# Another order of a layer's pieces, and another end of the recurrence, in a fused convolution-attention-recurrence kernel

## The chip, the cores and the metric

The kernel runs on one core of one Trainium2 chip. The metric is the device time of one execution in microseconds, as the median of several runs. The engines are TensorE (PE in the profile, its weight loads PEld), VectorE (DVE), ScalarE (ACT), GpSimd (POOL) and SyncE (SP, which here only issues transfers).

## The reference

The input x has 4 images of 128 channels and 64 x 64 pixels, all in float32. Two layers follow each other.

Layer 0 normalises over the channels, adds a 3 x 3 depthwise convolution with edge padding to the result, cuts each image into windows of 16 x 16, and lets each pixel of a window attend to its 5 x 5 neighbours, in two branches of four heads of 32 channels:

```
y = layernorm2d(x);  y = y + cpe(y)
q, k, v = per window and branch: Wq y, Wk y, Wv y
o = softmax over 25 neighbours (q . k_nb / sqrt(32)) . v_nb     # padding counts as zero logits
x = x + (Wo o of branch 0 + 0.5 * Wo o of branch 1) / sqrt(1.25)
```

Layer 1 takes the pixels as 4096 tokens of 128 features:

```
t = t + linear_attention(ln(t))      # elu + 1 features; cumulative sums over the tokens; num / den
t = t + ffn(ln(t)), where ffn is:
  Wx = x W^T, normalised per feature over all 4 * 4096 tokens, times gamma, plus beta
  y_t = sigmoid(Wx_t + V y_(t-1))    # a recurrence over the 4096 tokens of an image
```

The last normalisation needs the mean and the variance over all tokens of all images. So the recurrence can't begin until the last token's product is there.

## The kernel before

**Bands.** An image is worked in 4 bands of 16 rows (1024 tokens), 16 bands in all, and a band in 4 windows, 64 in all (`places`). The matmuls are float32, and each shows in the profile as two passes.

**Layer 0.** `norm_rows(n)` normalises a band's rows, turns them with TensorE and writes them into `ypad`. `convolve(n, half)` applies nine taps to two windows at a time, the first on ACT (L376), eight on DVE (L378), and copies the result to `y2w` on ACT (L414). Band 0 is different: `convolve_first` does windows 0 and 1 with taps on ACT and DVE, and `multiply_first` does windows 2 and 3 with matmuls against diagonal matrices (L396). A window then goes through `q`, `k`, `v` (L427, L440; `v` also sends two transfers, `v_sb`), `logits` (L467, L480, then four exponentials, L489), `sums` (L509, the softmax denominators; the copy `den`, L512, and the transfer `dc`), `values` (L524), `inverse` (DVE adds and inverts, L535 and L537, then the transfers `rd` and `rden` spread the result) and `scaled` (POOL, L552). `output0` (L578, L585) is the projection of half a band and needs all four windows of the band scaled.

**Layer 1.** Each band has two halves of 512 tokens. In the orders they are called `a` and `c`; the halves of the band before are `y` and `z` (in the last part `v` and `w` for the one before these). Per half the pieces are `output`, `measure`, `norm`, `turn`, `queries`, `keys`, `values`, `scores`, `turn_keys`, `accumulate` (the running state), `attend0`, `attend1`, `measure_last`, `send`, `spread`, `keep` and `product`. `send` and `spread` pass the second normalisation's factors through DRAM to all partitions. `keep` turns the result, copies it on ACT and stores it (L719). `product` multiplies by the recurrence's weights, and takes the statistics with DVE's `bn_stats` (L740) from `wx` in SBUF. The last half uses `norm_last` and `turn_last` in place of the factors (L616, L730).

**The order.** It is written out by hand. `START` writes out the order of pieces up to the fourth window. Then a loop goes through the windows with `SLOT`; numbers in it are gaps, and in the gaps of four windows the 24 entries of `LAYER1` are done one after the other, and steps of the next band's `front` (rows and taps) as `AHEAD` says. `TAIL` writes out what is left after the last window's logits. `warm.N` puts N matmuls on zeros ahead of the next piece that takes a PSUM bank. The order of the program is held on PE, DVE, ACT and POOL by `in_order()`; SP's queue isn't held by it. A piece that was done already is passed over:

```python
        if h is not None and name not in h.done:
            does[name](h)
            h.done.add(name)
```

**The recurrence.** Each image's 4096 tokens are cut into 128 segments of 32 steps, which run side by side as 512 columns; 11 steps ahead of the segment's own start, the first of them without a predecessor, make its first value. A step is three groups of columns: DVE seeds PSUM with the normalised product (L942), TensorE adds V y (L1004), ACT takes the sigmoid (L1009). The results of four steps make a block `ys`, from a ring of 3 buffers. For images 0 and 1 a block goes to the output by an accumulating transfer from POOL's queue (L1016), onto the residual that `keep` stored there. For images 2 and 3 the residual is loaded back (`res`, L913), added on POOL (L1022; the last step on DVE) and stored from SP's queue (L1028). At the end DVE compares segment ends with the warm-up's values (L1035), a flag is made from it (L1049), every engine loads it and branches (L1052, L1054) past a slower general version.

## Time and profile before

| | us |
|---|---|
| runs of the kernel before | 838.75, 839.15, 840.38; median 839.15 |
| the profiled execution's own time | 843.62 |
| its span | 841.80 |
| busy PE, DVE, ACT, POOL | 806.6, 693.2, 530.8, 254.2 |
| first layer 1 output (L578) | 72.0 |
| last window's logits done | 724.65 |
| first matmul of the recurrence (L1004) | 784.95 |
| last sigmoid begins | about 828.1 |

The profile is one execution; its times count from the span's start. A line such as L378 is a line of the kernel, and in a group `out<-in` names the tiles. What stands in square brackets after an instruction is the idle time of its engine before it and what ended it.

### The profile page before, as it was taken

The numbers are of one execution on the slowest core, as the hardware profiler recorded it, in microseconds if no ns is written. First come the engines' busy times: TensorE is split into PE (matmuls) and PEld (weight loads), VectorE is DVE, ScalarE is ACT, GpSimd is POOL, SyncE is SP. The second block draws the span as 40 slices with busy tenths as digits, with TensorE's granted clock in tenths as the row PEclk, the third lists the DMA queues.
The fourth block names the chain that finished last, engine by engine and source line by source line (L and its number), as shares of the span: only waits on it lengthen the run. The fifth ranks groups of instructions, "written<-read, shape, count | busy, mean of one in ns | idle before, by whom it ended". The sixth has DMA issues, their size and how long they took to land.

```text
span 841.8 us, 28915 instructions
## 1 busy us (share of the span) xinstructions
PE 806.6 (96%) x11803; PEld 642.3 (76%) x11805; DVE 693.2 (82%) x2127; ACT 530.8 (63%) x1026; POOL 254.2 (30%) x365
## 2 busy tenths in 40 slices
PE   6998999999999999999999999999999999988993
PEld 3766787878787878778787878787878878756792
DVE  6565989897989998998989898998999886466882
ACT  3675757676757576666767676757666665613782
POOL 2122232423233232413142323323332303121193
PEclk7999999999999999999999999999999999999997
DMA  4022141332323231414132232323141313121697
GB/s 140 18 64 70 42 113 42 79 79 66 91 68 97 57 103 36 109 42 119 40 86 75 62 87 67 96 65 98 39 108 39 92 41 95 44 56 38 209 224 174
DMA packets 81422, 68.81 MB, mean 82 GB/s; under 512 B 44800, under 2 KB 63872, under 8 KB 81280
## 3 DMA queue, kind: packets, MB, share of 16 engines
q1 hardware_dynamic: 53200, 43.47, 18.0%
q10 hardware_dynamic: 26928, 19.20, 9.2%
q0 software_dynamic: 1152, 4.19, 2.9%
q8 instruction: 95, 1.56, 0.8%
q14 instruction: 47, 0.39, 0.2%
HBM read 39.51 MB, written 17.89 MB: 68 GB/s over the span
## 4 chain that ended last, share of the span: by engine, by line
PE 86%; DVE 4%; DMA 4%; POOL 2%; ACT 1%; issue 1%; ACTq 0%; DVEq 0%; POOLq 0%; SPq 0%
PE bank L427 12%; PE bank L509 7%; PE bank L480 7%; PE bank L625 7%; PE bank L578 7%; PE bank L524 6%; PE bank L440 6%; PE bank L302 5%; PE bank L641 4%; PE z L1004 4%; PE bank L679 3%; PE bank L662 3%; PE bank L698 3%; PE bank L700 3%; PE bank L733 3%; PE bank L467 2%
## 5 line engine op out<-in xcount | busy, mean ns | idle before, releaser
L378 DVE SCALAR_TENSOR_TENSOR y<-ypad,cpe_w,y 128x512 f32<-128x512 f32 x240 | 191.7, 799 | 12.7 <-ACT y L376 7.7
L489 ACT ACTIVATE es<-bank 128x512 f32<-128x512 f32 x256 | 132.2, 604 | 32.1 <-PE bank L480 31.7
L285 POOL TENSOR_SCALAR rs<-mv 128x4 f32<-128x4 f32 (+2 forms) x100 | 25.3, 253 | 390.8 <-DVE mv L283 389.1
L552 POOL TENSOR_TENSOR oT<-o_sb,rden 128x512 f32<-128x512 f32 x64 | 83.0, 1297 | 119.1 <-DMA rden<-rd 104.2
L286 POOL TENSOR_TENSOR rs<-rs,mhalf 128x4 f32<-128x4 f32 (+2 forms) x100 | 106.0, 1060 | 8.3
L524 PEld LDWEIGHTS bank<-es,v_sb 128*32 128x32 f32 x3072 | 62.9, 110 | 39.2 <-issue 21.3
L480 PEld LDWEIGHTS bank<-q,k 32*64 32x64 f32 x4096 | 75.4, 130 | 2.7
L480 PE MATMUL bank<-q,k 32*64 32x96 f32 (+1 forms) x4096 | 77.5, 274 | 0.0
L512 ACT COPY den<-bank 128x512 f32<-128x512 f32 x64 | 37.4, 584 | 55.8 <-PE bank L509 55.3
L524 PE MATMUL bank<-es,v_sb 128*32 128x96 f32 (+1 forms) x3072 | 69.5, 237 | 1.6 <-DMA v_sb<-v_sb 1.6
L578 PEld LDWEIGHTS bank<-woT,oT 128*128 128x128 f32 x512 | 61.0, 196 | 13.2 <-POOL oT L552 9.6
L509 PE MATMUL bank<-es,ones 128*32 128x512 f32 x512 | 69.6, 605 | 0.6 <-ACT es L489 0.6
L427 PE MATMUL bank<-y2w,wqT 128*128 128x256 f32 x256 | 67.4, 386 | 2.4 <-DVE y2w L378 2.2
L625 PE MATMUL bank<-xl,awT 128*128 128x512 f32 x128 | 66.6, 607 | 0.0
L578 PE MATMUL bank<-woT,oT 128*128 128x128 f32 x512 | 62.3, 281 | 4.5 <-POOL oT L552 4.5
L427 PE MATMUL bank<-y2w,wkT 128*128 128x256 f32 x256 | 65.9, 380 | 0.0
L440 PE MATMUL bank<-wvT,y2w 128*128 128x256 f32 x256 | 65.9, 380 | 0.0
L535 DVE TENSOR_TENSOR dc<-dc,pad_c 128x32 f32<-128x32 f32 x64 | 25.5, 399 | 47.8 <-DMA dc<-den 47.7
L435 ACT COPY k<-bank 128x512 f32<-128x512 f32 x64 | 38.6, 603 | 41.2 <-PE bank L427 41.2
L627 ACT ACTIVATE low<-bank,minus 128x512 f32<-128x512 f32 x64 | 43.8, 685 | 24.5 <-PE bank L625 23.4
L427 PEld LDWEIGHTS bank<-y2w,wkT 128*128 128x128 f32 x256 | 47.3, 190 | 13.4 <-issue 7.5
L629 DVE SCALAR_TENSOR_TENSOR f<-low,bank 128x512 f32<-128x512 f32 x64 | 43.5, 680 | 16.6 <-ACT low L627 16.6
(131 smaller groups left out, 1687.9 us busy)
## 6 DMA issues: line engine op xcount, KB each, us to landing
rden<-rd SPq DMA_DIRECT2D x64, 256.0 KB
v_sb<-v_sb SPq DMA_DIRECT2D x128, 64.0 KB
factors<-factors ACTq DMA_DIRECT2D x31, 256.0 KB
xin<-in_xt SPq DMA_DIRECT2D x15, 512.0 KB
out<-rs_o ACTq DMA_DIRECT2D x16, 256.0 KB
resd<-rs_o ACTq DMA_DIRECT2D x16, 256.0 KB
out<-ot SPq DMA_DIRECT2D x32, 128.0 KB
out<-ys POOLq DMA_DIRECT2D x8, 512.0 KB, 7.4
```

What stands on the lines that cost most here:

```text
L286: nc.gpsimd.tensor_tensor(rs[:, :n], rs[:, :n], mhalf[:, :n], ALU.pow)
L378: nc.vector.scalar_tensor_tensor(y2, src, cpe_w[:, tap : tap + 1], y2, ALU.mult, ALU.add)
L427: nc.tensor.matmul(pps[:, br * WT : (br + 1) * WT], wT[:, br * P : (br + 1) * P], y2, start=True, stop=True,)
L440: nc.tensor.matmul(vps[:, e * 256 : (e + 1) * 256], y2[:, e * P : (e + 1) * P], wvT, start=True, stop=True,)
L480: nc.tensor.matmul(sps[h][half * KC : (half + 1) * KC, cols], w["k"][rows, k0 : k0 + KC], w["q"][rows, cols], start=False, stop=br == BR - ...
L489: nc.scalar.activation(es, sps[h], AF.Exp, scale=scale)
L509: nc.tensor.matmul(dps[rows], ones[:, :HD], w["es", h], start=True, stop=True)
L524: nc.tensor.matmul(ops[rows, cols], w["v"][:, n, c0 : c0 + HD], w["es", h][:, cols], start=(br, n) == pieces[0], stop=(br, n) == pieces[-1],)
L552: nc.gpsimd.tensor_tensor(oTs[n][:, :, :, wj * WS : (wj + 1) * WS], w["o"].rearrange("p (a r c) -> p a r c", a=BR, c=WS), w["rden"].rearra ...
L578: nc.tensor.matmul(yps[:, j * P : (j + 1) * P], oT[:, br, t], woT[:, br, :], start=br == 0, stop=br == BR - 1,)
L625: nc.tensor.matmul(zps, awT[:, m * P : (m + 1) * P], h.xl, start=True, stop=True)
L627: nc.scalar.activation(low, zps, AF.Exp, bias=minus)
```

## The change

Three things change. First, the order: `LAYER1`, one entry of `AHEAD`, `START` and `TAIL` are written anew, with the same pieces. In `LAYER1` values.a moves up beside queries.a, queries.c beside keys.c and attend1.a beside attend0.a, measure_last of the second half moves to the end of its own round, and keep.z stands ahead of norm.a. In `START`, `prepare` comes first, and the first parts of mul.2 and mul.3 stand ahead of q.0; there are 11 `warm` matmuls instead of 5. In `TAIL`, there are 14 instead of 13, scaled.63 and output.a come earlier, and product.z stands ahead of turn_last.c.

Second, the last statistics are taken from PSUM, ahead of the copy to `wx`, which DVE makes instead of ACT; the aggregate and the scale follow at once, and the shift takes one operation fewer.

Third, the last block of images 0 and 1 is not accumulated by the transfer. Its residual is loaded into `end_a`, DVE adds each of the last four steps to it, and ACT's queue stores it plainly. The ring of blocks has 4 buffers, and the last `ot` is added on POOL like the others.

```diff
@@ -41,55 +41,55 @@
 NA = B * NH // 2
 TOL = 5e-7
 LAYER1 = (
-    "measure_last.z",
+    "",
     "",
     "product.y send.z output.a",
     "measure.a spread.z output.c",
-    "norm.a",
-    "measure.c keep.z",
-    "",
-    "turn.a norm.c",
+    "keep.z norm.a",
+    "measure.c",
+    "turn.a",
+    "norm.c",
     "",
     "",
-    "keys.a product.z",
-    "turn.c queries.a",
-    "values.a",
-    "turn_keys.a scores.a keys.c",
-    "accumulate.a values.c",
-    "turn_keys.c attend0.a queries.c",
-    "attend1.a",
+    "queries.a values.a turn.c",
+    "product.z keys.a",
+    "turn_keys.a",
+    "scores.a keys.c queries.c accumulate.a",
+    "values.c",
+    "turn_keys.c attend0.a attend1.a",
+    "",
     "scores.c",
-    "measure_last.a",
-    "accumulate.c keep.a send.a",
+    "measure_last.a keep.a",
+    "accumulate.c send.a",
     "",
     "",
     "attend0.c spread.a attend1.c",
-    "",
+    "measure_last.c",
 )
 SLOT = ("sums", "values", "logits", 0, "scaled", "inverse", 1, "q", 2, 3, "k", "v", 4, 5)
-AHEAD = ("03", "01223345", "001245", "00234")
+AHEAD = ("03", "01223345", "001455", "00234")
 START = (
-    "warm.5 conv.0 prepare q.0 front conv.1 mul.2 mul.3",
-    "mul.2 k.0 front v.0 q.1 k.1 logits.0 front",
-    "q.2 front front front front mul.3 v.1 front",
-    "logits.1 sums.0 k.2 values.0 v.2 front front front",
-    "inverse.0 front front load.2 front logits.2 q.3 front",
-    "front sums.1 scaled.0 front values.1 inverse.1 q.4 k.4",
-    "sums.2 k.3 front front front v.3 scaled.1 logits.3",
-    "values.2 v.4 inverse.2 front front",
+    "prepare conv.0 front warm.3 mul.2 conv.1 mul.3 q.0",
+    "k.0 front front mul.2 v.0 q.1 k.1 front",
+    "logits.0 q.2 front front mul.3 front front v.1",
+    "sums.0 logits.1 front values.0 front front front k.2",
+    "inverse.0 scaled.0 v.2 front front load.2 front logits.2",
+    "front sums.1 front values.1 q.3 warm.6 sums.2 inverse.1",
+    "q.4 k.3 v.3 warm.2 front logits.3 scaled.1 front",
+    "values.2 inverse.2 front k.4 front v.4 front",
 )
 TAIL = (
-    "scaled.61 keep.w output.y send.w sums.63 spread.w output.z measure.z",
-    "measure.y inverse.62 norm.z values.63 product.w norm.y turn.y scaled.62",
-    "keys.y queries.y scores.y turn_keys.y inverse.63 turn.z values.z values.y",
-    "queries.z keys.z accumulate.y warm.1 attend0.y turn_keys.z product.v attend1.y",
-    "measure_last.y scores.z accumulate.z send.y spread.y attend0.z attend1.z keep.y",
-    "measure_last.z warm.2 send.z scaled.63 product.y warm.10 output.a measure.a",
-    "output.c measure.c norm.a spread.z keep.z turn.a norm.c turn.c",
-    "queries.a queries.c keys.a values.a keys.c turn_keys.a values.c scores.a",
-    "accumulate.a attend0.a attend1.a scores.c turn_keys.c measure_last.a accumulate.c keep.a",
-    "attend0.c send.a attend1.c measure_last.c spread.a keep.c norm_last.c product.a",
-    "turn_last.c product.z product.c",
+    "warm.2 warm.4 output.y keep.w send.w scaled.61 spread.w sums.63",
+    "measure.y output.z measure.z norm.z product.w norm.y warm.2 inverse.62",
+    "turn.z turn.y values.63 queries.y keys.y scores.y scaled.62 turn_keys.y",
+    "inverse.63 values.z values.y keys.z accumulate.y attend0.y queries.z turn_keys.z",
+    "attend1.y measure_last.y send.y product.v scaled.63 warm.3 spread.y accumulate.z",
+    "keep.y scores.z attend0.z attend1.z measure_last.z output.a send.z measure.a",
+    "product.y output.c measure.c norm.a turn.a keep.z norm.c values.a",
+    "keys.a turn.c warm.1 warm.1 spread.z queries.a warm.1 keys.c",
+    "turn_keys.a values.c scores.a accumulate.a attend0.a turn_keys.c queries.c attend1.a",
+    "measure_last.a scores.c accumulate.c keep.a attend0.c attend1.c send.a measure_last.c",
+    "spread.a keep.c norm_last.c product.a product.z turn_last.c product.c",
 )
 DGROUP = 4
 TINY, HUGE = 1e-30, 1e30
@@ -232,6 +232,9 @@
     stats = const.tile([P, B * T // 512, 6], F32, name="stats")
 
     wx = const.tile([P, B, NH, SEG, HSEGS], F32, name="wx")
+    mv = const.tile([P, 2], F32, name="mv")
+    sc = const.tile([P, 1], F32, name="sc")
+    shift = const.tile([P, 1], F32, name="shift")
 
     first = len(nc.cur_bb.bb.instructions)
 
@@ -728,7 +731,13 @@
         wps = bank()
         if h.factors is None:
             nc.tensor.matmul(wps, fwT, h.xl, start=True, stop=True)
-            nc.scalar.copy(wx[:, h.b, h.hb], wps.rearrange("p (k s) -> p s k", s=SEG))
+            nc.vector.bn_stats(stats[:, h.b * NH + h.hb, :], wps)
+            nc.vector.bn_aggr(mv, stats.rearrange("p n s -> p (n s)"))
+            nc.gpsimd.tensor_scalar(sc, mv[:, 1:2], 1e-5, 1.0, ALU.add, ALU.mult)
+            nc.gpsimd.tensor_tensor(sc, sc, mhalf[:, :1], ALU.pow)
+            nc.vector.tensor_scalar(shift, mv[:, 0:1], -1.0, None, ALU.mult)
+            nc.vector.tensor_copy(wx[:, h.b, h.hb], wps.rearrange("p (k s) -> p s k", s=SEG))
+            return
         else:
             nc.tensor.matmul(wps, fwT, h.rs.rearrange("p s k -> p (s k)"), start=True, stop=True)
             nc.vector.tensor_tensor(
@@ -901,29 +910,27 @@
 
     sp = fast.enter_context(tc.tile_pool(name="sp", bufs=1))
     rec = ExitStack()
-    ring = rec.enter_context(tc.tile_pool(name="ring", bufs=3))
+    ring = rec.enter_context(tc.tile_pool(name="ring", bufs=4))
     ZBUFS = 2
     ps_r = rec.enter_context(tc.tile_pool(name="ps_r", bufs=ZBUFS, space=PSUM))
     ps_m = rec.enter_context(tc.tile_pool(name="ps_m2", bufs=1, space=PSUM))
 
     res = sp.tile([P, B // 2, NH, SEG, HSEGS], F32, name="res")
+    end_a = sp.tile([P, NA, RUN, HSEGS], F32, name="end_a")
     for s0 in (0, SEG // 2):
         steps_of, cols = slice(s0, s0 + SEG // 2), slice(s0 * HSEGS, (s0 + SEG // 2) * HSEGS)
         for i, b in enumerate(resd):
             (nc.sync, nc.scalar)[i].dma_start(
                 res[:, i, :, steps_of].rearrange("p n s k -> p n (s k)"), resd[b][:, :, cols]
             )
-
-
-    mv = sp.tile([P, 2], F32, name="mv")
-    nc.vector.bn_aggr(mv, stats.rearrange("p n s -> p (n s)"))
-    sc = sp.tile([P, 1], F32, name="sc")
-    nc.gpsimd.tensor_scalar(sc, mv[:, 1:2], 1e-5, 1.0, ALU.add, ALU.mult)
-    nc.gpsimd.tensor_tensor(sc, sc, mhalf[:, :1], ALU.pow)
+    nc.sync.dma_start(
+        end_a.rearrange("p m r k -> p (m r k)"),
+        out_a[SEG // RUN - 1].rearrange("p m r k -> p (m r k)"),
+    )
+
+
     nc.vector.tensor_tensor(sc, sc, gamma, ALU.mult)
-    shift = sp.tile([P, 1], F32, name="shift")
-    nc.vector.tensor_tensor(shift, mv[:, 0:1], sc, ALU.mult)
-    nc.vector.tensor_tensor(shift, beta, shift, ALU.subtract)
+    nc.vector.scalar_tensor_tensor(shift, shift, sc, beta, ALU.mult, ALU.add)
 
 
     rounds = [(s, False) for s in range(SEG - WARM + 1, SEG)] + [(s, True) for s in range(SEG)]
@@ -1012,14 +1019,23 @@
         if not moved:
             last = ys[:, :, s % RUN, :]
         if counts:
-            if s % RUN == RUN - 1:
+            if s >= SEG - RUN:
+                nc.vector.tensor_tensor(
+                    end_a[:, :, s % RUN], end_a[:, :, s % RUN], last[:, :NA], ALU.add
+                )
+            elif s % RUN == RUN - 1:
                 nc.gpsimd.dma_start(
                     out_a[s // RUN].rearrange("p m r k -> p (m r k)"),
                     ys[:, :NA].rearrange("p m r k -> p (m r k)"),
                     accum_op=ALU.add,
                 )
+            if s == SEG - 1:
+                nc.scalar.dma_start(
+                    out_a[s // RUN].rearrange("p m r k -> p (m r k)"),
+                    end_a.rearrange("p m r k -> p (m r k)"),
+                )
             ot = ring.tile([P, COLS // 2], F32, tag="ot", name="ot", bufs=8)
-            (nc.vector if s == SEG - 1 else nc.gpsimd).tensor_tensor(
+            nc.gpsimd.tensor_tensor(
                 ot.rearrange("p (m k) -> p m k", k=HSEGS),
                 res[:, :, :, s, :].rearrange("p b n k -> p (b n) k"),
                 last[:, NA:],
```

## The prediction

> **What bounds the kernel now.** I read first the chain of work that ended last, by engine, then the busy time in stretches, then the chain and the timeline at the two ends.
>
> ```profile
> PE 86%; DVE 4%; DMA 4%; POOL 2%; ACT 1%; issue 1%; ACTq 0%; DVEq 0%; POOLq 0%; SPq 0%
> ```
>
> TensorE carries the chain. In stretches (columns: stretch, length, busy PE, weight loads, DVE, ACT, POOL, granted clock, DMA share, GB/s):
>
> ```profile
> 60.00:105.00 45.00, 41.33 (x634) 32.69 (x641) 31.84 (x98) 29.20 (x54) 12.33 (x17) 0.96 0.22 61
> 105.00:150.00 45.00, 45.00 (x729) 36.48 (x719) 40.22 (x125) 29.74 (x55) 13.54 (x20) 1.00 0.28 76
> ```
>
> From 105 to 690 us TensorE idles 0.75 us in all (585 us): it is the bound there, DVE a near second at 40 of 45. Idle TensorE lies at the ends: some 12 us before 72, 7.4 between 724 and 785. In the recurrence (785 to 828) matmul and sigmoid alternate.
>
> The start hangs on a chain of transfers (start, us, what):
>
> ```profile
> 59.40 0.58 ACT den L512
> ...
> 60.26 4.00 DMA dc<-den
> ...
> 66.43 4.13 DMA rden<-rd
> ...
> 70.69 1.27 POOL oT L552
> ...
> 72.00 5.47 PE bank L578 x32
> ```
>
> The first output projection (L578) waits 3.42 us for window 3's softmax divisors, and they start at 59.4 because the denominator's copy stands on ACT behind the y2w copy, which waits for DVE's last tap (timeline):
>
> ```profile
> 18.71 2.07 PE L427 MATMUL bank<-y2w,wqT 128*128 128x256 f32 x4 [2.18 <-DVE y2w L378]
> 20.58 6.38 PE L396 MATMUL bank<-ypad,wx 128*128 128x256 f32 x26
> ...
> 58.87 0.62 ACT L414 COPY y2w<-y 128x512 f32<-128x512 f32 x1 [2.85 <-DVE y L378]
> ```
>
> At the other end, from the timeline:
>
> ```profile
> 779.06 1.03 DVE L734 TENSOR_TENSOR wx<-bank,factors 128x512 f32<-128x512 f32 x1 [0.60 <-PE bank L733]
> 780.13 1.30 DVE L740 BATCH_NORM_STATS2 stats<-wx 128x6 f32<-128x512 f32 x2
> 781.52 1.02 DVE L919 BATCH_NORM_AGGREGATE mv<-stats 128x2 f32<-128x192 f32 x1
> ...
> 824.62 0.72 ACT L1009 ACTIVATE ys<-z 128x176 f32<-128x176 f32 x3 [1.33 <-DMA out<-ys]
> ```
>
> and, from the waits of SP's queue (us in total, times, longest):
>
> ```profile
> SPq L1054 <- SPq L1054: 3.4, 1, 3.4
> ```
>
> The recurrence loses 1.33 us to a ring buffer still being stored. From 805 to 835 the DMA share is 0.97 to 1.1; SP then waits 3.4 us for the last transfer (about 836.8), and the closing steps follow at 837.3, ending at 841.8.
>
> **What the Trainium skill says.** "TensorE: Matmul & The Clock Gate", section "What's actually happening": the array runs at half rate when idle, at full rate after about 3.4 us of sustained work. The trace agrees: four L427 passes take 2.07 us at 18.71 and 1.03 at 28.5; the clock reads 0.50 from 12 to 20 and 1.00 from 22. "DMA: Bandwidth & Descriptors", "SWDGE vs HWDGE vs iDMA": accumulating needs GpSimd's queue, plain stores run from ACT's; its section on the anatomy of one DMA fits 2.0 us plus bytes/436e3, an estimate of 3.2 us for 512 KB. The trace has 7.4 for the accumulating one, amid other traffic, and no plain one of that shape. "VectorE: DVE Perf Modes", section on the TRN2 errata: (120 + 512)/0.96 GHz = 0.66 us for a PSUM source (an estimate); the scores' PSUM multiply (L664) measures 0.65.
>
> **The change part by part.** Its sum is made against the profiled execution: 843.62 us, span 841.80. That is 4.47 above the median of 839.15; I carry the difference over.
>
> Start. (a) prepare moves ahead of conv.0. Its six DVE operations (0.22, 0.22, 0.29, 0.56, 0.56, 0.28 = 2.1 us) stood at 18.57 to 20.5, between the taps of conv.0 and conv.1. Now they fall into DVE's 2.37 us idle before 14.53, behind the cold matmuls L210 (1.49) and L217 (0.63) from 12.5; they end near 15.4, so conv.0 ends at 19.6 instead of 18.67. (b) The first 16 of 36 L396 matmuls (16 x 0.24 = 3.9 us) go ahead of the first queries, under conv.0's taps; the three fills there warm the clock. (c) conv.1 starts after 1.15 us of measuring: 20.8 to 24.9 (before 21.94 to 26.1). Then I walk the queues with the rows' durations. TensorE: q.0 from 20.0 (1.0), k.0 0.86, ten L396 2.4, v.0 0.86, q.1 when conv.1 ends (25.0), k.1, transposes once xf is scaled (27.2): first logits 27.7 (before 30.34). Logits 1.4, q.2, transposes, ten L396: 32.8, so band 1's first tap on ACT at 33.3 (36.48); its first half, eight DVE taps of 0.79 and one division of 0.6, done 41.1 (46.1). TensorE goes on with v.1, sums.0, logits.1, values.0, k.2, v.2, logits.2, sums.1 (8.3 us in all): window 1's sums end at 41.2, its denominator is copied at 43.2 behind four exponentials (2.06) and lands, after 2.5 to 3 us as at 47.26, at 46.3; then division, four taps, division, four taps: 53.9 (before 58.8). The denominator of window 3 leaves at 55.1 instead of 60.26; from there 11.7 us as now: L578 at 66.8 instead of 72.0. TensorE is there by 63.7, idles 3.1 and starts cold as it does now. The eight fills added (warm.6, warm.2: 1.9 us) lie under this chain. Gain 5.2 by hand; I book **4.5**, as a hand walk misses queue waits; bounds 1 to 6. What waits: DVE at each division, with the next taps queued behind it (counted); POOL at scaled.0 and scaled.1 for rden, with nothing behind until band 2 is measured; SP at rden for rd, with v_sb behind it as now. SP's order isn't written out: inside the bounds.
>
> Bands. LAYER1 and AHEAD reorder, with no instruction more. Tightest new neighbours: turn_keys.a, now first after logits. keys.a ends 3.3 us of TensorE earlier (sums 1.0, values 0.9, logits 1.4); ACT needs 0.69, DVE 1.76 for product.z and 0.68: about 1.7 us, slack 1.6. accumulate.a stands 2.6 us behind turn_keys.a; k1's copy waits for four exponentials (2.06) and takes 0.6: slack 0.6. norm.a to turn.a as before. measure_last.z (1.15 us DVE) leaves the fullest gap. Covered by TensorE's continuous work: **0**; bounds 0.7 gained (all idle there) and 9 lost (0.6 a band, 15 bands), as no trace shows these slacks.
>
> Tail, counted from the last logits' end (724.65). values.y has moved into the loop: 0.9 lost there, 0.9 less here. scaled.63 leaves its place behind measure_last.z on POOL (745.54, 20.9 us in): after measure_last.y's 1.3 us, near 15.7. So the last band's output starts at about 18.2 instead of 22.2, and norm.a, on DVE behind product.y (1.76), ends near 27.2 (before 29.1). TensorE has idled some 3.5 us by then, so values.a and keys.a run cold, as L625 did at 755 (0.66 clock): 1.9 us lost beside a warm walk. measure_last.c ends near 48.6 (before 49.6). Then product.z's matmuls stand ahead of turn_last: the 0.60 idle goes. Reading the last statistics from PSUM removes ACT's 0.58 copy from ahead of them, but DVE was still at product.z's statistics until 780.75 while the copy ended at 780.70: nothing more from that. The copy of wx moves to DVE (0.66) under POOL's 0.96 between aggregate and sc; bounds 0 to 0.3 lost. Two small operations after it instead of three: 0.19. Sum 1.0 + 0.6 + 0.1 + 0.19 - 0.9 = **1.0**; bounds -1.5 and 3.
>
> End. A fourth ring buffer: the block for s=28 takes the one of s=12 (stored from 811.59, landed by 820), not of s=16 (816.09 plus 8.43): 1.33 gone. Of eight accumulating stores (24.6 us of 16 engines by the queue's share, 3.05 each) seven stay; end_a's load (512 KB at the 350 GB/s of res: 1.5 us) falls where the DMAs idle (795 to 800, share 0.15) and stands on SP ahead of the first out<-ot, which goes only at 797.8; the plain store costs about 1.5. Four end_a additions (0.42 to 0.93 each on DVE, idle 0.24 in two steps) wait for each step's sigmoid with seeds queued behind them, and delay those by under 0.3 us, needed only a step later. ot of the last step goes to POOL (0.72 to 1.04), behind three others, while POOL loses the 0.87 us of issuing. Last sigmoid to flag stays 3.0. With the drain still the end, 3.05 - 1.5 = **1.5** comes off (it covers the 1.33: the drain would not move more); if the drain is not the bound, the flag's branch on TensorE (838.4, from 831.44) is, and up to 3.2 comes off. Bounds 0.5 and 3.2.
>
> Sum 4.5 + 0 + 1.0 + 1.5 = 7.0: profiled 843.6 - 7.0 = 836.6, median 839.15 - 7.0 = **832** (832.1).
>
> **The rivals.** More (0.20): the tail stays warm (1.9) and the drain isn't the bound (1.7): 10.6, near 828.5. For it: the warm fills in TAIL; against: none stands between output.c and turn.a. Less (0.13): the start's chain is refilled by SP or den's single buffer, half the 4.5 is left, and the tail gives 0: 839.15 - 2.25 - 1.5 = 835.4. No difference (0.07): the drain ends when it did, the start's chain too: 839. Slower (0.15): turn_keys.a or accumulate.a outruns DVE or ACT in each band. From 0.47 us a band (15 x 0.47 = 7) it eats the whole gain; at 0.6 it costs 9: 839.15 + 2 = 841. For it: DVE at 90% and in order, waiting 47.7 us in all for dc; against: DVE's load is evened out (its operations in the layer's first window sum to 11.4 us, before 12.6) and the old order had pairs as close. The forecast itself, 830.5 to 834, has 0.45.
>
> **How the numbers follow.** Faster by over 0.2%: 0.45 + 0.20 + 0.13 = 0.78; same 0.07; slower 0.15. (0.2%, 1.7 us, is about what a measurement of this kernel can tell from none.) The range of 8 in 10 is 827.5 to 841: it leaves out the far end of "more" and of "slower".
>
> **What would show it.** Right: L578 first at 66 to 68; TensorE idle under 1.5 us from 105 to 690; aggregate to first matmul about 0.2 us shorter; no wait of ACT for out<-ys; last sigmoid to end 12 to 13.4 us. Wrong: L578 after 70, or a new wait of TensorE at L654 or L679 in every band.

## The result, and the profile after

The changed kernel takes 837.47 us (median of 20 runs, 832.96 to 842.45) beside 842.01 for the kernel before on the same chip (20 runs, 838.75 to 846.09). The ratio is 0.9953, 95% interval 0.9939 to 0.9967. That is 4.0 us less, with 2.8 to 5.1 in the interval. The forecast was 7.0 less: the direction was right, the size was not. The absolute time is inside the range given, but the median of before is itself 2.9 us higher here than in the three runs shown earlier, so the ratio is the thing to judge.

The profiled execution took 836.31 us, span 834.6. It lies 1.2 below its median; the profiled execution of before lay 1.6 above the median of these 20 runs. The difference of the two profiles, 7.3 us, is therefore larger than the change is worth.

First the chain of work that ended last, by engine, in the profile of the kernel after:

```profile
PE 89%; DVE 5%; DMA 3%; POOL 1%; issue 1%; ACT 0%; SPq 0%; ACTq 0%; POOLq 0%; DVEq 0%
```

TensorE still carries the chain. Then the busy time in stretches of the kernel after (stretch, length, busy PE, weight loads, DVE, ACT, POOL, granted clock, DMA share, GB/s):

```profile
60.00:105.00 45.00, 41.42 (x651) 34.00 (x640) 35.39 (x113) 29.14 (x54) 12.52 (x17) 0.96 0.22 58
105.00:150.00 45.00, 45.00 (x717) 36.53 (x716) 40.68 (x128) 29.94 (x55) 13.91 (x19) 1.00 0.30 76
105.00:690.00 585.00, 585.00 (x9293) 473.46 (x9292) 521.02 (x1630) 393.91 (x712) 180.37 (x252) 1.00 0.28 75
```

From 105 to 690 us TensorE does not idle at all. A wait in every band, the rival on the slower side, would be seen here, and there is none.

The start, in the chain of the kernel after (start, us, what), as far as the first output projection:

```profile
52.81 0.62 ACT y2w L417
53.43 0.59 ACT den L515
...
55.19 4.21 DMA dc<-den
...
61.57 4.29 DMA rden<-rd
...
65.99 1.27 POOL oT L555
...
67.31 5.17 PE bank L581 x32
```

It is the same chain as before. The y2w copy has moved from 58.87 to 52.81, the denominator leaves at 55.19 instead of 60.26, and the projection begins at 67.31 instead of 72.00. (L578 of before is L581 here.)

The switch to the recurrence is the part that looks worse. In the timeline of the kernel before (start, us, engine, line, what; in brackets the idle time before it and what ended it) the zero matmuls that open the recurrence's PSUM banks (`fill`, L259 there, L262 here) ran without a wait:

```profile
781.45 1.48 PE L259 MATMUL z<-zeros 128*128 128x512 bf16 x6
...
784.95 1.08 PE L1004 MATMUL z<-ys,fvT 128*128 128x176 f32 x4
```

In the kernel after:

```profile
773.66 0.68 DVE L734 BATCH_NORM_STATS2 stats<-bank 128x6 f32<-128x512 f32 x1
774.38 1.02 DVE L735 BATCH_NORM_AGGREGATE mv<-stats 128x2 f32<-128x192 f32 x1
775.50 0.68 DVE L739 COPY wx<-bank 128x512 f32<-128x512 f32 x1
776.25 2.33 PE L262 MATMUL z<-zeros 128*128 128x512 bf16 x6 [2.53 <-DVE wx L739]
778.37 1.06 PE L262 MATMUL bank<-zeros 128*128 128x512 bf16 x2
779.22 1.04 PE L969 MATMUL bank<-mv,ident 128*128 128x256 f32 x2
780.97 1.28 PE L1011 MATMUL z<-ys,fvT 128*128 128x176 f32 x7
```

They wait 2.53 us, and what ends the wait is DVE's copy of wx. In the kernel before they started ahead of the aggregate (781.45 and 781.52), and took 1.48 instead of 2.33. From the aggregate's end (775.40) to the first matmul of the recurrence (780.97) it is 5.57 us; it was 2.41.

At the end, the wait of SP's queue for the last transfer, in the kernel after (us in total, times, longest):

```profile
SPq L1070 <- SPq L1070: 1.5, 1, 1.5
```

It was 3.4. ACT has no wait for out<-ys any more, and 11.83 us pass from the last sigmoid to the end (13.39 before; 12 to 13.4 were expected).

### The profile page after: what moved, and what is told of

The parts are those of the page before. It is cut to its first block, busy times and chain, and to the rows that moved or that the text cites. A ratio compares the mean times of both kernels' runs of the same rounds, so it can differ in the third digit from the quotient of the medians.

```text
span 834.6 us, 28916 instructions
## 1 busy us (share of the span) xinstructions
PE 804.1 (96%) x11806; PEld 643.1 (77%) x11812; DVE 690.3 (83%) x2131; ACT 531.3 (64%) x1025; POOL 255.0 (31%) x365
## 4 chain that ended last, share of the span: by engine, by line
PE 89%; DVE 5%; DMA 3%; POOL 1%; issue 1%; ACT 0%; SPq 0%; ACTq 0%; POOLq 0%; DVEq 0%
PE bank L430 13%; PE bank L483 8%; PE bank L512 7%; PE bank L581 7%; PE bank L628 7%; PE bank L443 7%; PE bank L527 7%; PE bank L305 6%; PE z L1011 4%; PE bank L644 3%; PE bank L701 3%; PE bank L682 3%; PE bank L665 3%; PE bank L703 3%; PE bank L742 3%; PE bank L470 3%
## 5 line engine op out<-in xcount | busy, mean ns | idle before, releaser
L381 DVE SCALAR_TENSOR_TENSOR y<-ypad,cpe_w,y 128x512 f32<-128x512 f32 x240 | 183.4, 764 | 16.5 <-ACT y L379 11.9
L581 PEld LDWEIGHTS bank<-woT,oT 128*128 128x128 f32 x512 | 60.9, 195 | 11.6 <-POOL oT L555 8.0
L581 PE MATMUL bank<-woT,oT 128*128 128x128 f32 x512 | 61.8, 279 | 3.6 <-POOL oT L555 3.6
L628 PE MATMUL bank<-xl,awT 128*128 128x512 f32 x128 | 64.0, 600 | 0.1
L538 DVE TENSOR_TENSOR dc<-dc,pad_c 128x32 f32<-128x32 f32 x64 | 23.5, 367 | 44.1 <-DMA dc<-den 43.9
L438 ACT COPY q<-bank 128x512 f32<-128x512 f32 x64 | 38.7, 605 | 27.7 <-PE bank L430 21.5
L284 DVE BATCH_NORM_STATS2 st<-x 128x6 f32<-128x128 f32 x256 | 55.4, 279 | 0.6
```

The lines of the kernel that those rows point to most:

```text
L381: nc.vector.scalar_tensor_tensor(y2, src, cpe_w[:, tap : tap + 1], y2, ALU.mult, ALU.add)
L438: nc.scalar.copy(w[name], pps)
L581: nc.tensor.matmul(yps[:, j * P : (j + 1) * P], oT[:, br, t], woT[:, br, :], start=br == 0, stop=br == BR - 1,)
L628: nc.tensor.matmul(zps, awT[:, m * P : (m + 1) * P], h.xl, start=True, stop=True)
```

## The experiments

All ratios are to runs of the kernel before on the same chip. To place a difference I cut each profile at the same marks; every column is in us. A single profile scatters by about 1 us in a column: of the rows with the old TAIL, the column up to the aggregate has 57.74, 56.07, 57.78 and 57.53. So I compare means, or runs that differ in one mark only. (The last logits end at 724.80 by this mark, not at the 724.65 given earlier; the spans are taken to 0.1 us.)

| kernel | ratio | first output projection | from it to the last logits' end | to the aggregate's end | to the first recurrence matmul | to the span's end |
|---|---|---|---|---|---|---|
| before | 1 | 72.00 | 652.80 | 57.74 | 2.41 | 56.85 |
| after | 0.9953 | 67.31 | 650.62 | 57.47 | 5.57 | 53.63 |
| e11, after again | 0.9957 | 65.81 | 651.36 | 57.13 | 3.90 | 53.80 |
| e1, copy on ACT | 0.9931 | 67.23 | 651.24 | 56.14 | 2.65 | 54.94 |
| e2, old statistics | 0.9911 | 67.09 | 651.02 | 55.71 | 2.36 | 55.52 |
| e12, copy first | 0.9933 | 67.87 | 651.48 | 56.41 | 3.73 | 54.31 |
| e8, ten more fills | 0.9944 | 66.79 | 652.36 | 56.23 | 3.89 | 55.43 |
| e7, statistics only | 1.0013 | 71.85 | 652.82 | 57.53 | 3.90 | 56.20 |
| e3, four tables only | 0.9926 | 66.45 | 652.01 | 57.08 | 2.41 | 56.05 |
| e5, START only | 0.9922 | 67.33 | 650.30 | 57.78 | 2.41 | 55.88 |
| e6, the other tables | 0.9983 | 72.86 | 652.90 | 56.12 | 2.85 | 54.47 |
| e4, new end only | 0.9995 | 72.76 | 651.87 | 56.07 | 2.37 | 55.13 |
| e9, see below | 0.9903 | 67.52 | 652.17 | 55.45 | 2.71 | 54.85 |
| e10, plain stores | 0.9888 | 66.95 | 652.30 | 56.38 | 2.37 | 51.70 |

**e1: DVE's copy of wx goes back to ACT.** The statistics stay in PSUM.

```diff
-            nc.vector.tensor_copy(wx[:, h.b, h.hb], wps.rearrange("p (k s) -> p s k", s=SEG))
+            nc.scalar.copy(wx[:, h.b, h.hb], wps.rearrange("p (k s) -> p s k", s=SEG))
```

> The changed kernel with one line different: ACT, not DVE, copies the last product to wx; the statistics still come from PSUM. Theory (bank switch): the zero matmuls on the recurrence's PSUM banks wait for the last reader of the product's banks; that was DVE's copy (ended 776.18 with the fills at 776.25) and is now DVE's statistics, 1.8 us earlier, so the first recurrence matmul comes 1 to 2 us earlier than in the changed kernel, counted from the last half's norm. Time about 5.5 us under the kernel before (ratio 0.9935). Rival (bands): the gain missing from the forecast was lost in the reordered bands and the runs' scatter, and the switch hides nothing: the first recurrence matmul stays where it was to 0.5 us, ratio 0.995.

Measured: ratio 0.9931 [0.9906, 0.9956]. From the timeline of e1:

```profile
773.59 0.59 ACT L739 COPY wx<-bank 128x512 f32<-128x512 f32 x1 [3.99 <-DVE stats L734]
...
774.22 1.47 PE L262 MATMUL z<-zeros 128*128 128x512 bf16 x6 [0.46 <-ACT wx L739]
```

The switch takes 2.65 us instead of 5.57; the fills wait 0.46 us, now for ACT's copy, and take 1.47. One line's engine decides the switch. By time alone the intervals of e1 and of the changed kernel overlap.

**e2: the whole statistics part undone; new order and new end stay.** The aggregate and the scale go back behind the bands.

```diff
-            nc.vector.bn_stats(stats[:, h.b * NH + h.hb, :], wps)
-            nc.vector.bn_aggr(mv, stats.rearrange("p n s -> p (n s)"))
...
-            nc.vector.tensor_copy(wx[:, h.b, h.hb], wps.rearrange("p (k s) -> p s k", s=SEG))
-            return
+            nc.scalar.copy(wx[:, h.b, h.hb], wps.rearrange("p (k s) -> p s k", s=SEG))
...
-    nc.vector.scalar_tensor_tensor(shift, shift, sc, beta, ALU.mult, ALU.add)
+    nc.vector.tensor_tensor(shift, mv[:, 0:1], sc, ALU.mult)
+    nc.vector.tensor_tensor(shift, beta, shift, ALU.subtract)
```

> The new order and the new end of the recurrence, but the last statistics as in the kernel before: ACT copies, DVE takes the statistics from wx, aggregate after the bands, three operations for sc and shift. Bank switch: the last reader is now product.z's DVE read or ACT's copy, about 3 us before the end of DVE's copy in the changed kernel; the fills run under statistics, aggregate and power, and the first recurrence matmul comes 2 to 3.5 us earlier than in the changed kernel, although the shift is ready 0.2 us later. Ratio about 0.992 (6.5 us under). Bands rival: 0.995, as the changed kernel. A third reading (cold clock): the fills and the small matmuls after them take 4.7 us in the changed kernel because TensorE runs at half rate there, 2.6 us in the kernel before; if the clock is the whole cause, the first matmul moves by under 1 us.

Measured: 0.9911 [0.9885, 0.9938], 7.5 us below the kernel before: what was forecast for the whole change. The interval stays just clear of that of the changed kernel (0.9939 to 0.9967), though not of that of its second measurement (e11, from 0.9934). The timeline of e2 at the switch, in the same columns:

```profile
769.83 0.59 ACT L734 COPY wx<-bank 128x512 f32<-128x512 f32 x1 [1.22 <-PE bank L733]
770.44 1.01 DVE L737 TENSOR_TENSOR wx<-bank,factors 128x512 f32<-128x512 f32 x1
...
771.59 1.46 PE L262 MATMUL z<-zeros 128*128 128x512 bf16 x6 [0.50 <-DVE wx L737]
772.80 1.02 DVE L926 BATCH_NORM_AGGREGATE mv<-stats 128x2 f32<-128x192 f32 x1
```

ACT has emptied the last product's bank at 770.4, so the fills wait only for DVE's reading of the other product (L737, to 771.45) and run under the last statistics and the aggregate. In the changed kernel they come after both, and after the copy.

**e7: the statistics part alone, on the kernel before** (the edit of e2 the other way round). The part doesn't save an operation on the shift: the mean's sign is turned ahead of the scale, so that one fewer stands behind it.

> The kernel before with the statistics of the change alone (taken from PSUM, aggregate at once, DVE copies wx, one operation fewer), old order and old end. Bank switch: the zero matmuls wait for DVE's copy here too; from the aggregate's end to the recurrence's first matmul 4.3 us if TensorE stays warm, 5.5 if it falls to half rate in the wait, against 2.4 before; time 2 to 3 us over the kernel before (1.002 to 1.0035). Forecast: 0.3 us under it (0.9997). Rival (cold clock): the loss in the changed kernel comes from TensorE idling after product.z was moved; with the old order there is no loss, 1.000.

Measured: 1.0013 [0.9998, 1.0028]; the fills wait 1.66 us for DVE's copy, and the switch takes 3.90. By itself the part costs 1.5 us in the profile and 1.1 (a gain of 0.2 to a loss of 2.4) by time, less than the 2 to 3 expected. By time the rival's 1.000 is inside the interval too; the wait in the profile is what speaks against it.

**e8: ten more zero matmuls ahead of the switch,** so that TensorE comes to it warmer.

```diff
-    fill(bank(), 6)
+    fill(bank(), 16)
```

> The changed kernel with 16 zero matmuls instead of 6 at the end of the bands, on a product bank, so that TensorE works through the wait for DVE's copy. It parts the switch's loss of 3.2 us in two: the wait itself stays (fills on the recurrence's banks still begin after the copy), the half rate goes. Expected from the aggregate's end to the first matmul: 5.6 us in the changed kernel, 4.0 to 4.3 here (six fills 1.5 instead of 2.3, two 0.6 instead of 1.06, the first of the three small ones 0.6 instead of 1.04). Ratio 0.9935. If the half rate costs nothing, 5.6 and 0.995.

Measured: 0.9944 [0.9925, 0.9963], switch 3.89, fills 1.48 after a wait of 1.74. This looks like the 1.7 us of half clock won back, but that isn't shown: e11, next, has the same 3.90 without those fills.

**e11: the changed kernel once more, unaltered.**

> The changed kernel once more, unaltered, as the base for the next run on the same chip. All theories: the ratio is again near 0.995 and the switch to the recurrence (end of the last aggregate to the first recurrence matmul) again takes 5 to 6 us, with the zero matmuls waiting some 2.5 us for DVE's copy of wx. If the 5.57 us of the first profile were chance, it would be 2.4 to 4 here.

Measured: 0.9957 [0.9934, 0.9979]. The switch takes 3.90 here. From its timeline:

```profile
773.28 1.02 DVE L735 BATCH_NORM_AGGREGATE mv<-stats 128x2 f32<-128x192 f32 x1
...
775.14 1.48 PE L262 MATMUL z<-zeros 128*128 128x512 bf16 x6 [2.00 <-DVE wx L739]
...
778.20 2.00 PE L1011 MATMUL z<-ys,fvT 128*128 128x176 f32 x12
```

So the wait belongs to the kernel, but the last 1.7 us of the 5.57, expected to return, belong to the first profile's execution. The granted clock says what they were: in stretches while the fills and the broadcasts run, the kernel after has 0.50,

```profile
776.70:779.70 3.00, 3.00 (x9) 1.45 (x8) 2.86 (x7) 1.37 (x3) 0.00 (x0) 0.50 1.07 350
```

and e11, in the same work, 1.00:

```profile
775.60:778.10 2.50, 2.50 (x13) 1.74 (x12) 2.36 (x6) 1.37 (x3) 0.00 (x0) 1.00 1.07 358
```

**e12: the copy stays on DVE, but stands ahead of the last statistics.**

```diff
+            nc.vector.tensor_copy(wx[:, h.b, h.hb], wps.rearrange("p (k s) -> p s k", s=SEG))
             nc.vector.bn_stats(stats[:, h.b * NH + h.hb, :], wps)
...
-            nc.vector.tensor_copy(wx[:, h.b, h.hb], wps.rearrange("p (k s) -> p s k", s=SEG))
```

> The changed kernel with one line moved: DVE's copy of wx out of the last product's PSUM bank stands ahead of that product's statistics instead of behind the aggregate and the shift. Theory (the zero matmuls that open the recurrence's banks wait for the bank's last reader): the last reader is now the statistics, done before the 1.02 us aggregate begins, so the zero matmuls run under it, the switch takes 2.4 to 2.8 us instead of 5.57, the aggregate ends about 0.7 us later, and about 2.4 us are won against the changed kernel: ratio near 0.9925. Rival (the loss is DVE's copy by itself, or another work of the switch on DVE): the copy's 0.68 us only changes its place, and the ratio stays at 0.995.

Measured: 0.9933 [0.9917, 0.995], near the 0.9925 of the theory; it is 0.0024 below e11 on the same chip, but the two intervals overlap. From the timeline of e12:

```profile
774.02 0.69 DVE L735 BATCH_NORM_STATS2 stats<-bank 128x6 f32<-128x512 f32 x1
774.74 1.02 DVE L736 BATCH_NORM_AGGREGATE mv<-stats 128x2 f32<-128x192 f32 x1
774.76 2.09 PE L262 MATMUL z<-zeros 128*128 128x512 bf16 x6 [2.74 <-DVE stats L735]
```

The fills now wait for the statistics, which have become the bank's last reader, and start with the aggregate instead of after it: the theory held. The switch, however, took 3.73 us and not 2.4 to 2.8. TensorE had idled 2.74 us, and its clock was at 0.50 from 775.5 to 778.9; from the first fill to the first matmul of the recurrence it took 4.73 us, where e11 took 3.06 at full clock.

**e3, e5 and e6: the order alone.** e3 is the kernel before with all four new tables, e5 with START only, e6 with LAYER1, AHEAD and TAIL only; nothing else differs.

> The kernel before with the four order tables of the change and nothing else. The forecast's steps: 4.5 us from the start, 0 from the bands, 1.0 from the tail, so 5.5 under the kernel before (0.9935), first output projection at 66.8 to 67.5 us, last logits about 6 us earlier. Bands rival: the time per band is longer than the 45.2 us of before by 0.1 us or more, and the ratio is 0.997 or above.

> The kernel before with the new START alone. The forecast's step: 4.5 us under the kernel before (0.9946), bounds 1 to 6, with the first output projection at 66.5 to 67.5 us instead of 72 to 72.8 and nothing changed from there on (752 us from it to the recurrence's last matmul within 1.5). Rival (given back later): the later stages, DVE above all, take up the time again, and the ratio is 0.998 although the first projection comes early.

> The kernel before with LAYER1, AHEAD and TAIL of the change and the old START. The forecast's steps: 0 from the bands, 1.0 from the tail, so 0.9988, within 0.9965 and 1.001. From the order-only run (6.2 us) less the start's 5 us: 1.2 us. Rival (bands pay): LAYER1 costs 0.1 us a band and the ratio is above 1.001.

Measured: e3 0.9926 [0.9900, 0.9953], e5 0.9922 [0.9891, 0.9953], e6 0.9983 [0.9967, 0.9999]. START by itself gives 6.6 us (4.0 to 9.2), the other three tables 1.4 (0.1 to 2.8), all four together 6.2.

**e4: the new end alone** (end_a, the ring of 4, the last ot on POOL, on the kernel before).

> The kernel before with the new end of the recurrence alone (end_a, plain store, ring of 4, last ot on POOL). Forecast: 1.5 us under the kernel before (0.998), up to 3.2 if the drain of transfers isn't the bound (0.996); no wait of ACT for out<-ys; last sigmoid to span end 12 to 13.4 us. The changed kernel's profile showed 1.66 us in the recurrence and 1.55 after it, so 3.2 if both are the end's own. Rival: the end brings nothing by itself (1.000), since what is saved was the later start of the transfers.

Measured: 0.9995 [0.9978, 1.0012]: 0.4 us less, from 1.9 less to 1.0 more. The interval holds the forecast's 1.5 and the rival's nothing alike, so by time e4 decides nothing. ACT's wait for out<-ys is gone. That wait is a matter of the execution: the five profiles with the old end have 1.33, 0.49, 0, 0.31 and 1.18 us of it (before, e3, e5, e6, e7).

**e9: e2, with the shift as in the change and layer 1's 256 KB store of half a moved behind the small transfer of the factors.** Of the edit against the changed kernel, the order alone:

```diff
-    "measure_last.a scores.c accumulate.c keep.a attend0.c attend1.c send.a measure_last.c",
-    "spread.a keep.c norm_last.c product.a product.z turn_last.c product.c",
+    "measure_last.a scores.c accumulate.c attend0.c attend1.c send.a measure_last.c",
+    "spread.a keep.a keep.c norm_last.c product.a product.z turn_last.c product.c",
```

> The changed kernel with the last statistics and the copy of wx as before the change (the copy on ACT, the statistics from wx), the shift in two operations, and keep.a moved behind spread.a in TAIL, so that layer 1's 256 KB store of segment a no longer stands just ahead of its 2 KB send. Theory (the send waits behind the store's transfer): the spread is issued 1.4 to 2 us after the send instead of 3.3 to 4.2, DVE's product.a no longer waits for factors (1.15 us in the version with the statistics as before), the aggregate ends about 54.6 us after the last logits instead of 55.7, and the ratio is about 0.990. Rival (the time from send to spread is that of the two instructions' queues, or the product waits for something else that ends at the same moment): the aggregate stays at 55.7 and the ratio at 0.991.

Measured: 0.9903 [0.9879, 0.9927], the lowest but for e10, though not separable from e2. The issues of the send (factors<-rs), of the 256 KB store (resd<-rs_o) and of the spread (factors<-factors), from the timeline of the kernel before,

```profile
770.87 0.32 SPq L609 DMA_DIRECT2D factors<-rs  x1
771.01 0.33 ACTq L719 DMA_DIRECT2D resd<-rs_o  x1
772.27 0.33 ACTq L620 DMA_DIRECT2D factors<-factors  x1
```

of the kernel after,

```profile
762.45 0.33 ACTq L722 DMA_DIRECT2D resd<-rs_o  x1
762.62 0.32 SPq L612 DMA_DIRECT2D factors<-rs  x1
766.78 0.33 ACTq L623 DMA_DIRECT2D factors<-factors  x1
```

and of e9:

```profile
763.68 0.32 SPq L612 DMA_DIRECT2D factors<-rs  x1
765.09 0.33 ACTq L623 DMA_DIRECT2D factors<-factors  x1
766.12 1.23 ACTq L722 DMA_DIRECT2D resd<-rs_o  x1
```

The spread can go once the send has landed: 1.40 us after it before, 4.16 in the kernel after, where the large store goes 0.17 us ahead of the send, and 1.41 with the store behind. DVE's product.a waits 1.80 us for the factors in the kernel after (1.15 in e2), and no longer in e9. But that is not what the theory promised further on: the aggregate ends 55.45 us after the last logits, not 54.6, near the rival's 55.7 and e2's 55.71. The wait is gone, and that the kernel gained by it isn't shown. Nor does a store ahead of the send always cost as much: in e6 it also goes 0.17 us ahead, and the spread follows after 2.00 us. The Trainium skill ("DMA: Bandwidth & Descriptors", section "Queues, rings and completion order") fits: each DMA engine takes turns between its queues a packet at a time, so a small transfer on SP's queue still shares the engines with a large one on ACT's. That it is this sharing, and not something else in the store, no run here tells apart.

**e10: e2 with the seven stores from POOL's queue plain.** It leaves out adding the residual of images 0 and 1 in the first 28 steps.

```diff
                     ys[:, :NA].rearrange("p m r k -> p (m r k)"),
-                    accum_op=ALU.add,
```

> The changed kernel with the last statistics and the copy of wx as before the change, and the seven stores of images 0 and 1 from GpSimd's queue plain instead of accumulating: it leaves out adding the residual of these images in the first 28 steps. Theory of the prediction (what is left of the transfers bounds the end): each accumulating store [...]takes the 16 DMA engines about twice as long, so with plain ones the recurrence and the end together fall from 55.5 us to about 54, the ratio from 0.991 to about 0.989. Rival (the path of the last instructions, branches and waits of the engines bounds it): the recurrence and the end together stay at about 55, the ratio at 0.991, although the DMA engines fall idle earlier.

Measured: 0.9888 [0.9854, 0.9922], about 2 us below e2, though the intervals overlap; recurrence and end together take 51.70 us in the profile, 3.8 less than in e2 and more than the 1.5 expected. From the first matmul to the end of the last sigmoid it is 42.28 us in both, so all of it lies behind the last sigmoid. POOL's queue (packets, MB, share of 16 engines) in the page of the kernel after,

```profile
q0 software_dynamic: 1008, 3.67, 2.5%
```

and in the page of e10:

```profile
q0 software_dynamic: 1008, 3.67, 1.1%
```

Per 512 KB store that is 2.98 us of the 16 engines accumulating (2.5% of 834.6 us, by seven) and 1.30 plain; from issue to landing the median is 7.2 and 3.5 us. The last stretches of e10 (columns as above):

```profile
815.00:823.25 8.25, 5.14 (x33) 4.41 (x32) 7.49 (x19) 4.69 (x17) 5.58 (x8) 1.00 0.73 265
823.25:829.70 6.45, 0.00 (x0) 0.00 (x0) 0.01 (x1) 0.00 (x0) 0.00 (x0) 0.57 0.09 22
```

and of the kernel before:

```profile
823.00:835.60 12.60, 4.23 (x26) 3.44 (x25) 4.34 (x14) 3.63 (x14) 5.29 (x7) 0.80 1.02 231
835.60:841.80 6.20, 0.00 (x0) 0.00 (x0) 0.00 (x0) 0.00 (x0) 0.00 (x0) 0.50 0.07 17
```

In both some 6 us follow once the DMA engines have gone quiet (share 0.09 and 0.07). In e10 they are no longer full throughout even before that (0.73), and the span's end moved with the moment they fell quiet. The waits of SP's queue at the end tell what bounds it. In e2 and in e10 (us in total, times, longest):

```profile
SPq L1068 <- SPq L1068: 2.3, 2, 1.4
```

```profile
SPq L1065 <- DVE bad L1062: 1.4, 1, 1.4
```

In the kernels before and after and in e2, SP waits for the last transfers (3.4, 1.5 and 2.3 us) after it has read the flag: there they bound the end. In e10 it waits for DVE's flag, set at 823.26, and its waits hold none for a transfer after that: there the path of the last instructions, the rival, has taken over. So the transfers bound the end in the changed kernel, the accumulating ones are their dear part, and with plain stores nothing of that wait is left.

## Why the prediction was right or wrong

**Start: right in its chain; its size at most a little short.** L578 was forecast at 66.8 and came at 67.31 (65.81 to 67.87 in the ten profiles with the new START). Against the mean of the four with the old one (72.37) the mean of the ten (67.04) is 5.3 us earlier, close to the 5.2 of the hand walk. The way from there to the last logits is a further 1.1 us shorter (652.60 to 651.49; in e5 alone 2.3), which the step did not have. By profiles that is 6.4 together with the loop, by e5's time 6.6 (4.0 to 9.2) for START, against the 4.5 booked. That 4.5 is inside the interval, and e5's six executions had more of the clock than those of before (below), so whether the discount for queue waits was needed stays open.

**Bands: right.** No wait in a band; TensorE is busy for 585.00 of 585 us. Whether values.y costs its 0.9 us in the loop the profiles don't settle: the stretch to the last logits is 0.1 us longer in e6 than in before, 1.3 longer in the new-START kernels with the new LAYER1 than in e5, which is one profile.

**Tail, the order: right in sign, over-sized.** Without its statistics and values.y terms the step promised 1.7 us (1.0 + 0.6 + 0.1) between the last logits and the aggregate. With the new TAIL the mean of seven profiles (after, e1, e2, e3, e6, e8, e11) is 56.55, with the old one (before, e4, e5, e7) 57.28: 0.7. One thing it had wrong is on record: it took the send's 1.4 us over from the old order and never asked what the new one puts just ahead of it on the queues. That this is the missing 1.0 isn't shown: with the store behind the send (e9) it is 55.45, but e2, with the store ahead, has 55.71. Half clock fell differently too: between the last logits and the recurrence the kernel before has two steps of 3.4 us of it, the kernel after four, e2 one.

**Tail, the statistics: this step failed.** In its words: "The copy of wx moves to DVE (0.66) under POOL's 0.96 between aggregate and sc; bounds 0 to 0.3 lost", with 0.19 gained behind it. The copy takes 0.68 and does lie under POOL's work; that part is right. But the step asked only who waits for wx. The copy is also the last reader of a PSUM bank, and the zero matmuls of the recurrence queue behind that reader, with the broadcasts (L969) and the first matmul of the recurrence behind them. The switch was to become 0.2 us shorter; it became 1.5 longer (2.41 to 3.90 in e7, e11) and 3.2 longer where the clock fell as well (5.57). e1 shows that the copy's engine decides it; e12, that the bank's last reader does. By time the part costs 3.5 us, with 1.0 to 6.1 as its interval (0.9953 less 0.9911, the two half-widths added in squares, of 841 us). The Trainium skill points at it: "Perfetto Trace Analysis", section "Matmuls", wants independent matmuls to rotate through PSUM banks so that one bank is emptied while the next is filled. Before the change the fills had no such wait (0.06 us); with the copy on DVE they wait 2.53.

Not all of the delay reached the end. By the table, aggregate to span's end is 59.20 us in the first profile of the changed kernel and 57.70 in the second (e11), but 57.59 in e1 and 57.88 in e2: in these, where the first matmul came late, what follows it was shorter, though not in e8 (59.32). Why is open.

Nor did the step ask what the wait does to the clock. The Trainium skill ("TensorE: Matmul & The Clock Gate", section "What's actually happening") puts the fall to half rate after an idle window of about 3.4 us, and lets this window run freely. The traces agree on the window: in each of the fourteen, up to the end of the recurrence, the clock changes only on a grid of 3.41 us, to within 0.01 us, and the grid lies differently in each execution. They don't agree that TensorE must be idle for so long. Half clock came after gaps of 2.53 and 2.74 us (after, e12), and in the kernel before at 775.88, ahead of a matmul that had waited only 1.62; after gaps of 1.66, 1.74 and 2.00 (e7, e8, e11) it did not come. So a gap's length alone doesn't tell, and whether the switch runs at half clock is in part luck: the same kernel had it (after) and hadn't (e11).

**End: mechanism right, a little over-sized.** From the first matmul of the recurrence to the span's end it is 55.9 us in the five profiles with the old end and 54.7 in the eight with the new one and accumulating stores: 1.2, against 1.5 forecast. In each of the thirteen SP still waits for transfers at the end, so they are the bound, as the step had it. How the 1.2 splits at the moment the DMA engines go quiet depends on the share that is called quiet. e4's time (0.4 less, at most 1.9) agrees with 1.2, with 1.5 and with nothing; e2 and e3, which differ in the end alone, lie 1.3 apart, within their intervals. One reading was wrong without effect: the flag does not stay at 3.0 us behind the last sigmoid but comes after 4.32 (3.2 to 4.8 in the eight with the new end); in the kernel after DVE still adds to end_a until 825.04, ahead of its comparisons. The 1.33 us of ACT's wait was right not to be counted on top.

**The sum.** By the profiles' means start and loop together give 6.4, the order of the tail 0.7, the end 1.2: 8.3, and e2, which has just these, measures 7.5 (5.2 to 9.7). Less the statistics part's 1.5 to 3.2, 5.1 to 6.8 is left, and the changed kernel measures 4.0 (2.8 to 5.1). So the steps' sizes add up only roughly; 7.0 was nearly right for a kernel without the statistics part.

Part of the 3.5 us between e2 and the changed kernel is clock. Over the 280 executions recorded with the experiments, each beside the mean of its own kernel and chip, the time grows by 0.64 us with each us of clock lost (time times one less the mean granted clock; correlation 0.74), and the six of e2 and of e5 had means of 0.986 and 0.987 where before had 0.983. An estimate at equal clock, by this slope: e5 gains 4.5 us (3.6 to 5.3), e2 5.9 (4.9 to 7.0), e11 4.3 (3.3 to 5.4), and e7 loses 1.2 (0.6 to 1.9). By it START gives what was booked, and the statistics part costs 1.2 to 1.6 us. It also takes out whatever clock a kernel costs by its own doing, so it is rather a lower bound for that part.

Of the rivals, "less", with its 3.75 us, came nearest in number but not in cause: neither its refilled start nor its tail of nothing happened. "Slower" and "no difference" are excluded. "More" is not what happened, though e10 shows that the end had more to give.

What no profile shows is the last part of the gap: the two profiled executions of the changed kernel took 836.31 and 833.80 us, 1.2 and 3.9 below their medians. How often the switch falls to half clock in the slower ones was not measured; their records have the mean clock of the whole execution only.

## What to carry to other kernels

When a copy out of PSUM changes its engine, cost two things: who waits for the copied data, and who waits for the bank. The second can be far away in the code, here the zero matmuls of the next stage; here an idle engine that empties the bank at once was worth more than a shorter chain on a busy one. And where a latency is taken over from the old order for a small transfer, look at what large transfer the new order puts just ahead of it.

## What the runs showed of the hardware

- An accumulating 512 KB store takes 2.98 us of the 16 DMA engines, the same store plain 1.30 (q0 of the kernel after and of e10).
- The send, issued 0.17 us after a 256 KB store on another queue, let the spread go only after 4.16 us in the kernel after (3.3 to 4.1 in seven more profiles, but 2.00 in e6), against 1.40 to 1.43 in the five profiles with the store behind it.
- Up to the end of the recurrence the granted clock changes only on a grid of 3.41 us, which lies differently in each execution. Half clock came after TensorE gaps of 1.62 (before, at 775.88), 2.53 and 2.74 us, and did not come after others of 1.66 to 2.00.
- From SP's last branch to the end of the span it takes 4.2 to 5.5 us in every kernel here.
